# Fewer warming matmuls, and first-normalisation statistics and Newton steps regrouped in the first attention steps

## The chip, the core and the metric

The kernel runs on one core of a Trainium2 chip. Its five engines work from queues of their own and in order: PE (TensorE, matrix products), DVE (VectorE), ACT (ScalarE), POOL (GpSimd) and SP (SyncE, which here only issues transfers). The metric is the device time of one execution in microseconds (us); of several executions the median is taken, and less is better. Names such as L464 are lines of the kernel before.

## The reference

The input `x` has 16 batches of 128 tokens with 512 features. What is computed, cut to what matters:

```python
x = x + xattn(layernorm(x), ctx, ctx)      # 32 query heads, 8 key/value heads of 16
x = x + moe(layernorm(x), gate_weight, ...)# 32 experts, 8 per token, plus a shared expert

def layernorm(x):                           # over the 512 features, no weights
    return (x - mean(x)) / sqrt(var(x) + 1e-5)

def xattn(q, k, v):                         # per batch: 128 queries, 128 keys
    weights = softmax(q k^T / sqrt(16))
    return weights v
```

The mixture of experts routes every token of the second normalisation to 8 of 32 experts (sigmoid gate, groups), each with `silu(x w1) * (x w3)` times `w2`.

## The kernel before, in words

The kernel has two stages. In `attention_small` the 16 batches go through cross-attention and both normalisations; it takes roughly the first 124 us. In `experts` the tokens are routed, gathered by expert, multiplied and added to the output; it takes the rest, and in it PE is busy almost without a break.

All of PE, DVE, ACT and POOL run an order that is written out by hand: the instructions of an engine are executed in the order in which the Python code emits them, and an instruction that waits holds up all behind it on its engine.

The attention is cut into 32 items, two per batch: item `(b, i)` is half `i` of the heads of batch `b`. A loop over `n` from 0 to 31 emits one step per item. In a step PE does, in this order: the scores of item `n` (`sc`, L464, four matmuls into two PSUM tiles of which there are two buffers in all, so the scores of the next item need both exponentials of this one); the values of item `n - 1` (`oT`, L480); and transposes into one PSUM tile `x` (L434): the queries of the next batch in even steps, the second normalisation's rows in later steps, and the attention output of item `n - 2` (`oTs`). ACT takes the exponentials (`p`, L474, two per item) and copies the transposed queries out (`qT`, L455; for batches 0 and 1 DVE does that). DVE copies `oT` out (`oTs`, L489), divides by the sum of the softmax (`ri` L498, `at` L500) and so frees the tile `x`; POOL adds `at` to `x` of the batch (L507).

The first normalisation of batch `b` has three parts, which all have to be done before its queries are transposed:

- `layernorm_stats`: mean and variance on DVE, two instructions (`st` L91, `mv` L92);
- `layernorm_rstd(first, n)`: one over the square root for `n` batches at once by Newton steps, nine tiny instructions on DVE (L98 to L116) or twelve on POOL (L98 to L128);
- `rows_of`: the normalised rows `xq` on DVE (L132).

Three dictionaries say where such work is put in a step: `head[n]` ahead of the scores, `middle[n]` just ahead of the reading (on DVE and POOL) of the last set of transposes of that step, `tail[n]` at its end. The same three hold the second normalisation (its statistics of batch `b` at the end of step `2b + 4`), the keys (`keys`, ACT), and the values (`fixed_values`, two memsets of a tile `va`, and `values_of`, a copy into it).

Ahead of the loop there is the front: `x` of batch 0 is loaded in two halves, its statistics, Newton steps and rows follow on DVE (without a break between them), then its queries are transposed and step 0 begins. While this goes on, PE has no work of its own and multiplies a tile of zeros, `wz`, by itself: `keep_warm(WARM)` ahead of the first transposes, `keep_warm(FILL[-1])` between the transposes and the scores of item 0, and `keep_warm(FILL[0])` in step 0. One warming matmul (L329) is two records in the profile.

At the end of the attention, between about 106 and 124 us, the last batches pass one after the other through DVE and PE, and PE has gaps; then the experts begin.

Of the kernel before, what the change touches and what calls it, by code (L numbers as in the profile page):

```python
# [38 lines left out]
ORDER += [r for k in range(6) for r in (5 + k, 12 + k)]  # L39
ORDER += [*range(19, 29), 30, 31]  # L40
BIG = 32768
WARM = 18
FILL = {-1: 4, 0: 3}


@with_exitstack
def tile_xattn_moe(
# [15 lines left out]
    nc = tc.nc  # L63
    B, S, D = x.shape
# [24 lines left out]
    def layernorm_stats(b, norm):  # L89
        st = xnp.tile([P, 6], F32, tag="st", name="st")  # L90
        nc.vector.bn_stats(st, xs[b])  # L91
        nc.vector.bn_aggr(mv[:, norm[b], :], st)  # L92
# [58 lines left out]
    FIRST = [*range(12), *range(15, 18), 21]  # L151
# [125 lines left out]
    def attention_small():  # L277


        with ExitStack() as ph:  # L280
# [46 lines left out]
            def keep_warm(n):  # L327
                for _ in range(n):
                    nc.tensor.matmul(warm, lhsT=wz, rhs=wz, start=True, stop=True)  # L329

            keep_warm(WARM)
            nc.scalar.activation(table, table, AF.Exp)
# [63 lines left out]
            def rows_of(b):  # L396
                xqs[b] = ap2.tile([P, G, KV, HD], F32, tag="xq", name="xq")
                normalized(
                    xqs[b].rearrange("p g k d -> p k g d"),
                    xs[b].rearrange("p (k g d) -> p k g d", g=G, d=HD),  # L400
                    b,
                    FIRST,
                )
# [2 lines left out]
            layernorm_stats(0, FIRST)  # L406
            layernorm_rstd(0, 1)
            rows_of(0)
            layernorm_stats(1, FIRST)
            for i in range(2):  # L410
                keys(0, i)
            values_of(0)
# [6 lines left out]
            def transposes(*sets, pool=ps_x, between=()):  # L419


                x = pool.tile(
                    [P, 2, 2, 2, P], F32, tag=("x" if pool is ps_x else "sc"), name="x"
                )
                for s, (of, split, _) in enumerate(sets):
                    for k in range(4):
                        for h, rows in enumerate(halves):
                            if split:
                                to = x[:, h, :, s, ts(k, P // 4)]
                                by = ident[rows, rows].rearrange("p (a b) -> p a b", a=2)  # L430
                            else:
                                to = x[:, h, k // 2, s, ts(k % 2, H)]
                                by = ident[rows, rows]
                            nc.tensor.matmul(  # L434
                                to,
                                lhsT=of[rows, k, :],
                                rhs=by,
                                start=True,
                                stop=True,
                                is_transpose=True,  # L440
                                tile_position=(h * H, 0),
                            )
                for s, (_, _, then) in enumerate(sets):
                    if s == len(sets) - 1:
                        for f, a in between:
                            f(*a)
                    then(x[:, :, :, s])

            def queries(b):

                xn = xqs.pop(b).rearrange("p g k d -> p g (k d)")

                def then(x):
                    qTs[b] = ap2.tile([P, 2, 2, P], F32, tag="qT", name="qT")
                    (nc.scalar.copy if b > 1 else nc.vector.tensor_copy)(qTs[b], x)  # L455

                return xn, False, then
# [108 lines left out]
            head, middle, tail = {}, {}, {}  # L566

            def at(where, n, f, *a):
                where.setdefault(n, []).append((f, a))


            for b in (2, 3):
                at(head, 0, layernorm_stats, b, FIRST)
            at(tail, 0, layernorm_rstd, 1, 3)
            at(tail, 0, rows_of, 1)
            at(tail, 1, rows_of, 2)
            for b, n in ((4, 1), (5, 1), (6, 2), (7, 2)):
                at(tail, n, layernorm_stats, b, FIRST)
            at(head, 3, layernorm_rstd, 4, 4, nc.gpsimd)
            for b, n in zip(range(8, B), range(3, 18, 2)):  # L580
                at(middle, n, layernorm_stats, b, FIRST)
            for b in range(3, B):
                at(middle, 2 * b - 4, rows_of, b)

            at(head, 3, fixed_values, 1, nc.gpsimd)
            at(head, 4, keys, 1, 0)
            at(head, 5, keys, 1, 1)
            at(head, 5, values_of, 1)
# [20 lines left out]
            for b in range(11):  # L609
                n = min(2 * b + 13, b + 21)  # L610
# [10 lines left out]
            transposes(queries(0))  # L621
            keep_warm(FILL[-1])
            for n in range(N):
# [22 lines left out]
                else:  # L646
                    assert not between
                keep_warm(FILL.get(n, 0))
                if n in sums:
# [967 lines left out]

    pieces = [(k, i) for k in range(NTB) for i in range(NI)]
    left_over = attention_small()
    experts(pieces[1:], in_order, *left_over)  # L1620
    left = nc.values_load(
# [64 lines left out]
```

## Time and profile before

| | |
|---|---|
| median of 3 runs | 991.97 us (991.03 to 993.17) |
| the profiled execution | 985.66 us |
| its span, first to last instruction | 983.9 us |
| PE busy | 965.7 us (98%) |
| DVE, ACT, POOL busy | 288.6, 296.8, 486.7 us |
| mean granted clock of PE | 0.991 |

The profiled execution lies 6.3 us below the median of the three timed runs; sums are made against the profiled execution, and a difference found there is taken over to the median. A profile line gives an engine's instruction with its line, its output and inputs, and the number of records; in a timeline, brackets hold the idle time of the engine before it and what ended that. PEclk is the clock that was granted to PE, as a share of full speed. "<-" in a name separates what is written from what is read.

### The profile page before, as it was taken

The page shows a single profiled execution, that of the slowest core. Times are in us where ns is not written, and L with a number is a line of the kernel's source. Part 1 is how long each engine was busy: PE and PEld are TensorE (multiplying, and loading weights), DVE is VectorE, ACT ScalarE, POOL GpSimd, SP SyncE. Part 2 cuts the span into 40 slices and gives each one's busy share as a digit, 9 for nine tenths or more (in the row PEclk, how much of TensorE's full clock was granted, in tenths as well). Part 3 has the DMA queues.
Part 4 walks back from the last instruction along what each step waited for, and adds up shares of the span by engine and source line. Part 5 has one row for each costly group of instructions (what it writes and reads, how often), then busy time and mean ns, then how long its engine had stood idle before and what let it go on. Part 6 is the DMA issues. An engine that isn't in the chain of part 4 may idle for free.

```text
span 983.9 us, 13941 instructions
## 1 busy us (share of the span) xinstructions
PE 965.7 (98%) x4985; PEld 548.5 (56%) x4985; DVE 288.6 (29%) x972; ACT 296.8 (30%) x468; POOL 486.7 (49%) x597
## 2 busy tenths in 40 slices
PE   9999899999999999999999999999999999999996
PEld 5344444547666556666666676767654444444453
DVE  7877778961121111111112111111121112111100
ACT  6788513412222222222222222222222222222221
POOL 3577244753454446444547454545463444555443
PEclk9999799999999999999999999999999999999998
DMA  9011206145666658676769676757685776677543
GB/s 322 15 44 44 76 2 215 43 156 157 131 152 135 164 121 201 159 159 132 180 134 222 131 180 129 181 129 179 135 209 123 170 180 159 146 167 167 114 65 46
DMA packets 59869, 137.15 MB, mean 139 GB/s; under 512 B 12168, under 2 KB 16392, under 8 KB 59792
## 3 DMA queue, kind: packets, MB, share of 16 engines
q0 software_dynamic: 32032, 69.25, 37.9%
q1 hardware_dynamic: 27680, 66.81, 20.0%
q8 instruction: 41, 0.67, 0.3%
q14 instruction: 36, 0.29, 0.1%
q10 hardware_dynamic: 80, 0.13, 0.0%
HBM read 96.71 MB, written 46.73 MB: 146 GB/s over the span
## 4 chain that ended last, share of the span: by engine, by line
PE 84%; issue 5%; POOL 4%; DMA 3%; DVE 2%; ACT 1%; POOLq 0%; ACTq 0%; DVEq 0%
PE gu L1494 41%; PE y L1548 21%; PE gu L258 6%; PE trx L1446 4%; PE sc L464 4%; DMA out_dram<-yw,token 3%; POOL out_dram L1520 3%; PE oT L480 3%; PE y L1339 2%; PE x L434 2%; PE tok L1006 1%; DVE st L91 0%; PE lg L556 0%; PE lgT L541 0%; DMA x<-in_x_dram 0%
## 5 line engine op out<-in xcount | busy, mean ns | idle before, releaser
L1494 PE MATMUL gu<-xnT,wup 128*128 128x256 f32 (+27 forms) x1664 | 490.5, 444 | 0.0
L1494 PEld LDWEIGHTS gu<-xnT,wup 128*128 128x128 f32 x1664 | 314.4, 190 | 192.9 <-issue 133.5
L1520 POOL DMA_INDIRECT out_dram<-yw,token x150 | 234.8, 1565 | 347.3 <-ACT yw L1557 237.7
L1548 PE MATMUL y<-wdn,sa 128*128 128x512 f32 (+2 forms) x672 | 263.3, 599 | 0.0
L1505 DVE TENSOR_TENSOR sa<-sl,gu 128x256 f32<-128x256 f32 (+27 forms) x104 | 52.2, 502 | 623.6 <-PE gu L1494 618.3
L1557 ACT ACTIVATE yw<-y,wt 128x512 f32<-128x512 f32 x138 | 94.9, 687 | 243.8 <-PE y L1548 206.1
L1422 POOL DMA_INDIRECT xg<-rows,token x138 | 142.3, 1031 | 46.6 <-issue 27.8
L1548 PEld LDWEIGHTS y<-wdn,sa 128*128 128x128 f32 (+2 forms) x672 | 98.0, 170 | 94.4 <-issue 85.0
L1503 ACT ACTIVATE sl<-gu 128x256 f32<-128x256 f32 (+27 forms) x104 | 46.7, 449 | 250.2 <-PE gu L1494 250.2
L474 ACT ACTIVATE p<-sc 128x1024 f32<-128x1024 f32 x64 | 62.1, 1024 | 14.5 <-PE sc L464 14.5
L1462 ACT COPY xnT<-trx 128x512 f32<-128x512 f32 x69 | 37.2, 589 | 89.8 <-PE trx L1446 89.8
L258 PE MATMUL gu<-xnT,sup 128*128 128x512 f32 x128 | 60.5, 615 | 0.7 <-ACT ssl L266 0.7
L1000 POOL TENSOR_SCALAR hq<-slice_q,sq 128x138 f16<-128x138 f16 x32 | 35.2, 1113 | 36.3 <-DVE sq L1305 20.1
L1446 PEld LDWEIGHTS trx<-ident,xg 64*128 64x128 f32 x1104 | 37.2, 138 | 17.8 <-issue 17.5
L464 PE MATMUL sc<-qT,kz 32*128 32x512 f32 x256 | 43.9, 640 | 0.2 <-ACT p L474 0.2
L1446 PE MATMUL trx<-ident,xg 64*128 64x64 f32 x1104 | 42.1, 226 | 0.0
L1462 DVE COPY xnT<-trx 128x512 f32<-128x512 f32 x57 | 39.3, 689 | 5.6 <-PE trx L1446 4.8
L507 POOL TENSOR_TENSOR x<-x,at 128x256 f32<-128x256 f32 x29 | 21.3, 739 | 38.2 <-DVE at L500 36.0
L258 PEld LDWEIGHTS gu<-xnT,sup 128*128 128x128 f32 x128 | 23.4, 194 | 25.0 <-issue 22.5
L480 PE MATMUL oT<-p,va 128*32 128x512 f32 x256 | 34.3, 608 | 2.0 <-DVE oTs L489 2.0
L1477 DVE SCALAR_TENSOR_TENSOR own<-expert,owner,xg 128x32 f32<-128x32 f32 x138 | 31.2, 245 | 0.0
L1339 PE MATMUL y<-sdn,sa 128*128 128x512 f32 x64 | 29.6, 597 | 0.0
(190 smaller groups left out, 462.6 us busy)
## 6 DMA issues: line engine op xcount, KB each, us to landing
wup<-in_w_dram SPq DMA_DIRECT2D x64, 512.0 KB, 5.2
wdn<-in_w_dram SPq DMA_DIRECT2D x32, 512.0 KB, 5.1
rows<-xn SPq DMA_DIRECT2D x16, 256.0 KB, 2.0
out_dram<-x SPq DMA_DIRECT2D x16, 256.0 KB, 2.3
x<-in_x_dram SPq DMA_DIRECT2D x15, 256.0 KB, 5.6
out_dram<-yw,token POOLq DMA_INDIRECT x150, 5.0
xg<-rows,token POOLq DMA_INDIRECT x138, 4.4
cTs<-in_cT_dram SPq DMA_DIRECT2D x4, 256.0 KB, 4.6
```

The costliest lines, as they stand in the source:

```text
L258: nc.tensor.matmul(acc, lhsT=sup[:, w, d, ts(i, P)], rhs=xnT[k][:, d, :], start=(d == 0), stop=(d == ND - 1),)
L464: nc.tensor.matmul(scs[j // 2][:, j % 2], lhsT=kzs[b // 4 % 2][rows, b % 4, i, :], rhs=qT[rows], start=True, stop=True, tile_position=(j * ...
L474: nc.scalar.activation(p, sc, AF.Exp, scale=1.0 / HD**0.5)
L480: nc.tensor.matmul(oT[j * HP : (j + 1) * HP], lhsT=vas[b // 4 % 2][:, b % 4, 2 * j + i, :], rhs=ps.pop((b, i, j)), start=True, stop=True, ...
L1422: nc.gpsimd.indirect_dma_start(out=t, out_offset=None, in_=rows[:, :], in_offset=bass.IndirectOffsetOnAxis(ap=token[:, j : j + 1], axis=0) ...
L1446: nc.tensor.matmul(trs[s // 2][:, h, s % 2, d, :], lhsT=xg[j][rows_of_half, ts(d, P)], rhs=ident[rows_of_half, rows_of_half], start=True, ...
L1462: copy(xnT[n % NTB][:, :, col : col + P].rearrange("p d (h t) -> p h d t", h=2), tr)
L1494: nc.tensor.matmul(acc[:, 0:m], lhsT=wup[k % NW][:, w, d, ts(i, P)], rhs=xnT[n % NTB][:, d, 0:m], start=(d == 0), stop=(d == ND - 1),)
L1505: nc.vector.tensor_tensor(acts[n % NTB][:, i, 0:m], banks[2][:, 0:m], acc[:, 0:m], ALU.mult)
L1520: ins = nc.gpsimd.indirect_dma_start(out=flat, out_offset=bass.IndirectOffsetOnAxis(ap=token2[:, k - 1 : k] if a else token[0:b, j : j + 1 ...
L1548: nc.tensor.matmul(y[c0:c1, :], lhsT=acts[n % NTB][:, i, col : col + c1 - c0], rhs=wdn[pieces[n][0] % NW][:, i, :], start=(i == 0), stop=( ...
L1557: nc.scalar.activation(yws[j], y, AF.Copy, scale=wt[:, j : j + 1])
```

## The change

Four things are changed, all in the front and the first eight steps of the attention:

- `WARM` goes from 18 to 15 and `FILL[-1]` from 4 to 2.
- Statistics of the first normalisation: batch 1 moves from the front (between the rows of batch 0 and the copy of its queries) to the head of step 0, behind that copy; those of the batches after it, two to a step before, are spread, mostly one to a step.
- Newton groups: before, batches 1 to 3 on DVE at the end of step 0 and 4 to 7 on POOL at the head of step 3. Now batches 1 and 2 on DVE at the end of step 0, 3 and 4 on POOL at the head of step 2, and 5 to 7 on POOL at the head of step 5. (Groups after that, at step 10 and later, stay.)
- The rows of batch 3 move from step 2 to step 3, and the two memsets of the second `va` tile on POOL from the head of step 3 to the head of step 1.

```diff
-WARM = 18
-FILL = {-1: 4, 0: 3}
+WARM = 15
+FILL = {-1: 2, 0: 3}
...
             layernorm_stats(0, FIRST)
             layernorm_rstd(0, 1)
             rows_of(0)
-            layernorm_stats(1, FIRST)
             for i in range(2):
                 keys(0, i)
...
-            for b in (2, 3):
+            for b in (1, 2):
                 at(head, 0, layernorm_stats, b, FIRST)
-            at(tail, 0, layernorm_rstd, 1, 3)
+            at(tail, 0, layernorm_rstd, 1, 2)
             at(tail, 0, rows_of, 1)
             at(tail, 1, rows_of, 2)
-            for b, n in ((4, 1), (5, 1), (6, 2), (7, 2)):
-                at(tail, n, layernorm_stats, b, FIRST)
-            at(head, 3, layernorm_rstd, 4, 4, nc.gpsimd)
-            for b, n in zip(range(8, B), range(3, 18, 2)):
+            for b in (3, 4):
+                at(tail, 1, layernorm_stats, b, FIRST)
+            at(head, 2, layernorm_rstd, 3, 2, nc.gpsimd)
+            at(tail, 2, layernorm_stats, 5, FIRST)
+            for b, n in zip(range(6, B), (3, 4, 5, 7, 8, 9, 11, 13, 15, 17)):
                 at(middle, n, layernorm_stats, b, FIRST)
+            at(head, 5, layernorm_rstd, 5, 3, nc.gpsimd)
             for b in range(3, B):
-                at(middle, 2 * b - 4, rows_of, b)
-
-            at(head, 3, fixed_values, 1, nc.gpsimd)
+                at(middle, max(2 * b - 4, 3), rows_of, b)
+
+            at(head, 1, fixed_values, 1, nc.gpsimd)
```

In the built program DVE has the same instructions in the attention as before, in another order; PE has five warming matmuls less; POOL has one Newton group, twelve instructions, more.

## The prediction

> **What bounds the kernel now.** I read the page's busy shares first. PE is busy 98% of the span and the chain that ended last runs through PE for 84% of it. A saving in another engine therefore counts only where PE stands idle for it. The change touches only the front and steps 0 to 7 of the attention, so I next asked where PE is idle there, in the table of windows (columns: stretch, its length, then busy time and records of PE, PEld, DVE, ACT, POOL, then PEclk, DMA share, GB/s):
>
> ```profile
> 0.57:3.98 3.41, 2.89 (x13) 2.90 (x14) 1.57 (x6) 1.49 (x2) 2.79 (x15) 1.00 0.51 152
> 3.98:7.40 3.42, 2.76 (x25) 2.57 (x23) 2.79 (x13) 1.01 (x2) 1.62 (x15) 1.00 0.93 286
> ...
> 20.00:28.00 8.00, 7.29 (x76) 3.03 (x80) 7.19 (x17) 6.32 (x9) 5.50 (x18) 1.00 0.58 232
> 30.00:34.00 4.00, 4.00 (x32) 1.24 (x30) 3.47 (x10) 2.88 (x4) 0.73 (x1) 1.00 0.02 4
> 106.38:109.80 3.42, 1.47 (x24) 0.41 (x19) 3.11 (x13) 0.43 (x2) 1.68 (x1) 1.00 0.17 65
> 109.80:113.21 3.41, 3.17 (x32) 2.38 (x28) 2.88 (x8) 1.29 (x3) 2.58 (x2) 0.50 0.26 94
> ...
> 205.37:208.78 3.41, 2.52 (x13) 1.13 (x12) 3.41 (x13) 1.75 (x2) 0.80 (x2) 1.00 0.23 89
> ```
>
> From 30 us on PE is never idle; between 20 and 28 us it is, by 0.71 us, while DVE is nearly full. The last three rows matter for the clock: after a stretch of 3.42 us with PE busy 1.47 (43%) the clock fell to half; after one with 2.52 (74%) it did not. The first two rows show the clock opening: 13 warming records in 2.89 us (0.22 us each), then 24 or 25 in 2.76 (0.11 each), although the column says 1.00 in both.
>
> Then the timeline, PE first, DVE and POOL after it, shows which waits these are:
>
> ```profile
> 1.09 5.65 PE L329 MATMUL warm<-wz 128*128 128x128 f32 x36 [1.09 <-DVE wz L198]
> 7.59 0.47 PE L434 MATMUL x<-ident,xq 64*128 64x64 f32 x8 [0.86 <-DVE xq L132]
> 7.99 1.16 PE L329 MATMUL warm<-wz 128*128 128x128 f32 x8
> 9.08 1.14 PE L464 MATMUL sc<-qT,kz 32*128 32x512 f32 x8
> ...
> 22.99 0.46 PE L434 MATMUL x<-ident,xq 64*128 64x64 f32 x8 [0.24 <-DVE at L500]
> ...
> 26.24 0.47 PE L434 MATMUL x<-ident,oTs 64*128 64x64 f32 x8 [0.48 <-DVE at L500]
> ```
> ```profile
> 8.09 0.18 DVE L92 BATCH_NORM_AGGREGATE mv<-st 128x2 f32<-128x6 f32 x1
> 8.19 0.66 DVE L455 COPY qT<-x 128x512 f32<-128x512 f32 x1
> ...
> 24.35 1.13 DVE L132 TENSOR_SCALAR xq<-x,mv,rstd 128x512 f32<-128x512 f32 x1 [0.63 <-POOL rstd L128]
> ```
> ```profile
> 24.12 0.20 POOL L128 TENSOR_TENSOR rstd<-h,r 128x4 f32<-128x4 f32 x1
> 24.25 0.95 POOL L354 MEMSET va<- 128x1024 f32 x1
> ```
>
> DVE stands 0.63 us until POOL has finished its Newton group of four batches, and then its rows take 1.13 us, not the 0.55 of the other rows, beside POOL's memset. PE's waits of 0.24 and 0.48 us for `at` hang on DVE's queue there. All idle time of PE from the first warming matmul to 30 us, the 0.86 in the front included, is 2.0 us (1.3 in the stretch from 7.40 to 30, the rest ahead of it). That caps what the change can bring.
>
> **The parts, one by one.**
>
> *Warming ahead of the transposes, 18 to 15.* Six records less at 0.112 us: PE stops at 6.07, not 6.74. The first transposes wait for the rows (6.90 to 7.46), so the wait grows from 0.86 to 1.5 us and nothing is gained here: 0. It gains where the clock opens later than 3.98. If it is still slow at 7.40, 18 matmuls have done 29.6 of 36 records at 0.213, the other 6.4 end at 8.1, and the transposes are 0.5 late; 15 end at 7.5 and are not late. So 0 to -0.5; I take -0.1, since only openings after about 6.2 count.
>
> *Warming ahead of the first scores, 4 to 2, with the statistics of batch 1 moved.* Four records less, 0.45 us. The last warming record starts at 8.87 and the scores follow at 9.08, although `qT` was there at 8.85; `qT` itself began at 8.19, behind the aggregate of batch 1. Without both: transposes end at 8.06, the copy starts about 0.05 later (8.11), ends at 8.77, and PE follows a DVE result after 0.14 (7.46 to 7.59): scores at 8.91. -0.17, on the path.
>
> *Statistics of 1 and 2, Newton of 1 and 2 on DVE.* DVE does two statistics, nine Newton instructions (0.195 us apart, the same for two columns as for three) and the rows, as before, from 8.68 instead of 8.76: rows of batch 1 end at 12.74 instead of 12.82. PE wants them at 13.3 less 0.17. Cost 0; cover 0.35 us.
>
> *Statistics one a step.* Ahead of `at` of step 3, DVE now has statistics 5 and 6 instead of 6, 7 and 8, but the rows of batch 3, formerly in step 2, stand there. From the first `oT` of batch 1 (PE ends it at 19.98): `oTs` from 20.05, pitch 0.60; statistics 0.79; rows 0.46; `ri` 0.27; `at` 0.42: end at 22.59 instead of 22.84, all less the 0.17. PE's `oT` ends at 22.76 less 0.17. So the wait of 0.24 goes.
>
> *Newton of 3 and 4 on POOL.* Statistics 3 and 4 end where 4 and 5 ended, 17.58 less 0.17; twelve instructions 0.285 us apart make 3.4: ready at 20.9, wanted by the rows at 21.3. The 0.63 wait and the 0.58 of stretching go. `at` of step 4 then ends near 25.2, before PE's `oT` (25.76 less 0.41): PE's 0.48 goes as well. But the scores after it need the second exponential, which ended at 26.80 and moves only by 0.41, to 26.4; with a score pair of 1.07 the step ends at 27.5 instead of 27.99. So of the 0.48 only some 0.07 stays: what is late next is the exponential.
>
> *Newton of 5 to 7 on POOL, step 5.* This adds a wait. POOL reaches it after adding `at` of step 4, at about 26.0, and ends at 29.4; the rows of batch 5, at 29.66 before, are due at 29.2. DVE stands 0.2 to 0.3 us, with `ri`, `at` and the copies behind it; POOL's copy into `va` (0.62) comes right after and may stretch the rows by up to 0.4 (a row at 24.35 was stretched by 0.58). Cover: 0.32 us of DVE idle ahead of `ri` at 30.52, and PE takes `at` only 0.6 us after its end there. I take 0; without the cover +0.3.
>
> *Memsets of `va` on POOL, now behind its constants.* These end at 5.87; 0.95 us, then the small one from about 6.92, just as the rows of batch 0 start at 6.90, on the path. Its own time is 0.09 (on DVE) to 0.32 (on POOL). 0 to +0.35; I take +0.1.
>
> Sum: -0.10 - 0.17 - 0.24 - 0.07 + 0.10 = -0.48. The profiled execution of 985.66 becomes 985.2; the median of 991.97, 6.3 above it, becomes 991.5. The experts' stage, bound by PE, hands the shift on unchanged. About 0.2% (2.0 us) is what a measurement of this kernel tells from no change; the three timed runs alone lie 2.1 apart.
>
> The Trainium skill, "TensorE: Matmul & The Clock Gate", Part 1, says that PE's clock opens after about 3.4 us of sustained work and falls back only after an idle window of that length, the windows running free. By that rule the longer pause of 1.5 us costs nothing and the sum stays -0.48. The rows above speak against it: the clock fell after a window that was 43% busy.
>
> **Rivals.**
>
> *The clock closes in the front (slower).* With 15 matmuls PE is busy 2.09 us of the window 3.98 to 7.40: 61%, between the 43% that closed it and the 74% that did not. If it closes at 7.40, the first scores cost 1.07 more, fills and transposes some 0.3: +1.4, with the gain +0.9, 992.9. If it stays for a second window, as at 109.80, another score pair of 1.07: +2.0, 994.0. It decides from a threshold above 61%. For it: nearer evidence is lacking; against: 61% is nearer to the 74%, and the edges lie elsewhere in other executions. Chance 0.14.
>
> *The gain is eaten by POOL.* The Newton group of 5 to 7 and the memset both turn up at their upper bounds (+0.3 and +0.25 over what I took): 991.9 to 992.1. For it: POOL has twelve instructions more, and my due time and ready time lie 0.2 apart the wrong way. Chance 0.20.
>
> *The shift meets the later closing better (faster).* The clock steps at 109.80 and 120.04 lie 31 and 34 windows of 3.413 us after 3.98, so it switches on a grid. Of three half-speed windows after the attention one may fall away when the gap at 107 to 109 us moves or the executions differ: a window of some 3.2 us busy at half clock is worth 1.6, with the gain -2.1: 989.9. It is as likely to go the other way in single runs. Chance 0.11.
>
> **How the numbers follow.** My forecast has 0.55: 991.5. Its bounds are -1.2 (late opening -0.5, and the front's memset at nothing, and a little more of the 0.48) and +0.3, to which the runs' own scatter of 1.1 either way adds. The range reaches to 989.8, where the faster rival lies, and to 993.4, past the clock closing for one window. Faster by over 0.2% needs under 990.0: 0.09 from the forecast by scatter, 0.02 from POOL's case, 0.09 from the grid: 0.20. Slower needs over 994.0: 0.03, 0.04, and 0.09 from the clock: 0.16. The rest is 0.64.
>
> **What would show it.** After: scores of item 0 at 8.9; no wait of DVE for `rstd` at step 4 and no row of 1.13 us there; no wait of PE for `at` at 23 and 26 us; a short wait of DVE for `rstd` near 29 us; PE without a gap from there; the scores of step 8 (32.31 before) near 31.9. Wrong would be: PEclk 0.5 before 15 us, rows of batch 0 longer than 0.9 us, or PE waiting for `at` near 32 us.

## The result: 0.15% faster, just below the range

| | before | after |
|---|---|---|
| median of 20 executions each | 990.85 us (987.47 to 993.19) | 989.12 us (986.51 to 993.14) |
| mean of the 20 | 990.76 | 989.37 |
| the profiled execution | 985.66 | 990.59 |
| its span | 983.9 | 988.7 |
| mean granted clock of PE in it | 0.991 | 0.990 |

The ratio of after to before is 0.9985 (95% interval 0.9974 to 0.9995), about 1.5 us; the means lie 1.4 us apart, the medians 1.7. The forecast was 991.5 with a range from 989.8; the measured median lies 0.7 below its foot. The sign was right, the size (-0.48) was not.

The profiled execution of after is not a typical one: at 990.59 it lies in the upper part of its twenty. So the traces are compared stage by stage and not by their ends.

**The front and the first steps, after.** The timeline of PE, to be read against that of before (lines of after are numbered one lower):

```profile
1.09 6.12 PE L329 MATMUL warm<-wz 128*128 128x128 f32 x30 [1.09 <-DVE wz L198]
7.28 0.47 PE L433 MATMUL x<-ident,xq 64*128 64x64 f32 x8
7.68 0.71 PE L329 MATMUL warm<-wz 128*128 128x128 f32 x4
8.62 1.14 PE L463 MATMUL sc<-qT,kz 32*128 32x512 f32 x8 [0.23 <-DVE qT L454]
...
22.30 0.46 PE L433 MATMUL x<-ident,xq 64*128 64x64 f32 x8
...
25.14 0.46 PE L433 MATMUL x<-ident,oTs 64*128 64x64 f32 x8
25.53 1.76 PE L463 MATMUL sc<-qT,kz 32*128 32x512 f32 x8
...
28.22 0.47 PE L433 MATMUL x<-ident,xq 64*128 64x64 f32 x8
```

The brackets of 0.24 and 0.48 us "<-DVE at" are gone at 22.30 and 25.14. The scores of item 6, which took 1.35 us before, take 1.76: they start earlier and wait inside for the second exponential. Scores of item 0 come 1.34 us after the first transposes (8.62 less 7.28); before it was 1.49 (9.08 less 7.59). In this execution 30 warming records last until 7.2 us, where the 36 of before stopped at 6.74, because the clock opened only at 6.38.

The timeline of DVE and that of POOL, the same stretch:

```profile
6.59 0.55 DVE L132 TENSOR_SCALAR xq<-x,mv,rstd 128x512 f32<-128x512 f32 x1
...
23.78 0.52 DVE L132 TENSOR_SCALAR xq<-x,mv,rstd 128x512 f32<-128x512 f32 x1
...
29.21 0.80 DVE L132 TENSOR_SCALAR xq<-x,mv,rstd 128x512 f32<-128x512 f32 x1 [0.17 <-POOL rstd L128]
```
```profile
5.77 0.95 POOL L354 MEMSET va<- 128x1024 f32 x1
6.78 0.44 POOL L355 MEMSET va<- 128x32 f32 x1
...
28.98 0.19 POOL L128 TENSOR_TENSOR rstd<-h,r 128x3 f32<-128x3 f32 x1
29.12 0.61 POOL L358 COPY va<-cn 128x512 f32<-128x512 f32 x1
```

DVE no longer stands at step 4 and the rows of 1.13 us there are 0.52. The new wait for the group of 5 to 7 is there, 0.17 us, with rows of 0.80 behind it. The rows of batch 0 take 0.55 beside the small memset, as they did without it.

The table of windows (stretch, its length, busy us and records of PE, PEld, DVE, ACT, POOL, then PEclk, DMA share, GB/s):

```profile
20.00:28.00 8.00, 7.99 (x72) 2.88 (x72) 7.49 (x20) 6.96 (x10) 4.13 (x13) 1.00 0.51 206
30.00:34.00 4.00, 4.00 (x33) 1.17 (x32) 3.40 (x10) 3.38 (x4) 1.71 (x3) 1.00 0.00 0
105.37:108.78 3.41, 1.46 (x26) 0.47 (x20) 3.10 (x13) 0.41 (x2) 1.61 (x1) 1.00 0.16 59
108.78:112.19 3.41, 3.31 (x34) 2.38 (x28) 2.82 (x8) 1.22 (x3) 2.64 (x2) 0.50 0.25 94
...
221.42:224.83 3.41, 0.92 (x4) 0.84 (x5) 0.69 (x1) 1.07 (x2) 1.14 (x2) 1.00 0.80 300
224.83:228.24 3.41, 3.41 (x9) 2.73 (x9) 0.00 (x0) 0.38 (x1) 0.00 (x0) 0.50 0.28 85
```

Between 20 and 28 us PE is busy 7.99 us, 7.29 before. At the end of the attention the half clock comes again, after a window 43% busy, as before.

**Where the profiled time went.** The scores of step 16 start at 55.26 (56.19 before), and the first routed matrices of the experts were still to come when a stall put this execution back. The timeline of PE and that of ACT there:

```profile
223.91 5.41 PE L1495 MATMUL gu<-xnT,wup 128*128 128x256 f32 x16 [3.86 <-ACT xnT L1463]
```
```profile
222.78 1.07 ACT L1463 COPY xnT<-trx 128x512 f32<-128x512 f32 x2 [14.65 <-remote]
```

PE waits 3.86 us for ACT, and ACT, DVE and POOL all start again within 0.3 us of 222.8, released by a signal whose sender the profile does not know ("<-remote"); the window before it was 27% busy, so one at half clock follows. It cost 5.8 us: at the ninth record of the shared expert this execution was 0.95 ahead of before's (124.94 against 125.89), at the end 4.85 behind. None of the sixteen later traces has it, ten of them with the regrouping, so I count it as no part of the change; what sent the signal stays open. The twenty executions of either kernel lie some 5 us above the later ones of the same kernel (990.85 against 985); whether most of them had such a stall no trace shows.

### The profile page after: what moved, and what is told of

Same layout as the page of the kernel before. It is cut to its first block, busy times and chain, and to the rows that moved or that the text cites. A ratio compares the mean times of both kernels' runs of the same rounds, so it can differ in the third digit from the quotient of the medians.

```text
span 988.7 us, 13933 instructions
## 1 busy us (share of the span) xinstructions
PE 968.0 (98%) x4975; PEld 549.7 (56%) x4975; DVE 289.1 (29%) x972; ACT 296.6 (30%) x468; POOL 488.7 (49%) x609
## 4 chain that ended last, share of the span: by engine, by line
PE 86%; issue 4%; POOL 3%; DMA 3%; another core or an unknown queue 1%; DVE 1%; ACT 1%; POOLq 0%; ACTq 0%; DVEq 0%
PE gu L1495 42%; PE y L1549 21%; PE gu L258 6%; PE sc L463 4%; PE trx L1447 4%; PE oT L479 3%; DMA out_dram<-yw,token 3%; POOL out_dram L1521 3%; PE x L433 2%; PE y L1340 1%; PE tok L1007 1%; PE lg L555 0%; PE lgT L540 0%; ACT p L473 0%
## 5 line engine op out<-in xcount | busy, mean ns | idle before, releaser
L258 PE MATMUL gu<-xnT,sup 128*128 128x512 f32 x128 | 60.4, 614 | 0.7 <-ACT ssl L266 0.7
L1463 DVE COPY xnT<-trx 128x512 f32<-128x512 f32 x57 | 39.3, 689 | 31.9 <-PE y L1549 21.8
L258 PEld LDWEIGHTS gu<-xnT,sup 128*128 128x128 f32 x128 | 23.4, 194 | 25.0 <-issue 22.3
```

The costliest lines, as they stand in the source:

```text
L258: nc.tensor.matmul(acc, lhsT=sup[:, w, d, ts(i, P)], rhs=xnT[k][:, d, :], start=(d == 0), stop=(d == ND - 1),)
L1463: copy(xnT[n % NTB][:, :, col : col + P].rearrange("p d (h t) -> p h d t", h=2), tr)
```

## Experiments

From one series to the next the median of before differs (990.85 above, 984.87 to 985.91 below), so each result is compared with runs of before in its own series, on the same chip. "Filled" kernels have more warming matmuls at the end of the attention (the edit of e4). From each trace's timeline I took five marks: when the clock opened; how much later than its rows allow the first transposes began ("late"; rows' end and 0.14); transposes to first scores; scores of item 2 to scores of item 16; and the "gap", from the scores of item 30 to the ninth record of the shared expert (`gu`, L258). From there to the end every trace takes the same time to within 0.4 us (858.0), but for the stall above. "1 + 1" means two half-clock windows with an open one between them.

| | opened | late | transposes to scores | item 2 to 16 | gap | half-clock windows in the gap |
|---|---|---|---|---|---|---|
| before | 3.98 | 0 | 1.49 | 41.50 | 25.30 | 3 |
| after | 6.38 | 0 | 1.34 | 41.03 | 25.30 | 3 |
| e1 after | 6.15 | 0 | 1.35 | 41.03 | 24.94 | 1 + 1 |
| e2 warming only | 4.33 | 0 | 1.39 | 41.48 | 23.64 | 1 |
| e3 regrouping only | 6.63 | 0.76 | 1.49 | 41.04 | 26.55 | 1 + 2 |
| e4 after, filled | 5.72 | 0 | 1.33 | 41.04 | 22.58 | 0 |
| e5 before, filled | 7.31 | 0.99 | 1.48 | 41.49 | 22.58 | 0 |
| e6 regrouping, filled | 5.75 | 0 | 1.48 | 41.04 | 22.59 | 0 |
| e7 after, filled | 6.39 | 0 | 1.34 | 41.03 | 22.59 | 0 |
| e10 before | 5.15 | 0.01 | 1.48 | 41.48 | 24.25 | 1 |
| e11 after | 4.96 | 0 | 1.34 | 41.04 | 25.78 | 2 |
| e12 warming, filled | 7.18 | 0.20 | 1.35 | 41.48 | 22.58 | 0 |
| e13 before, filled | 6.13 | 0.23 | 1.48 | 41.49 | 22.58 | 0 |
| e14 after, filled | 4.14 | 0 | 1.34 | 41.05 | 22.59 | 0 |
| e15 before | 5.94 | 0.31 | 1.48 | 41.50 | 25.71 | 2 |
| e16 after | 3.94 | 0 | 1.34 | 41.02 | 23.90 | 2 |

### The two halves of the change, and its end (first series)

**e1** is after, unchanged, for a second trace. **e2** is before with the warming of after (statistics of batch 1 stay in the front), **e3** is after with the warming of before:

```diff
 e2, on before                     e3, on after
-WARM = 18                        -WARM = 15
-FILL = {-1: 4, 0: 3}             -FILL = {-1: 2, 0: 3}
+WARM = 15                        +WARM = 18
+FILL = {-1: 2, 0: 3}             +FILL = {-1: 4, 0: 3}
```

**e4** is after with warming matmuls in the gap at the end of the attention, meant to keep the clock from closing there. This filling is used in several runs below:

```diff
             gate_parts(8)
+            warm = ps_sc.tile([P, 2, TB], F32, tag="sc", name="warm2")[:, 0, 0:P]
+            keep_warm(8)
             values(*items[N - 1])
...
             gate_sums(8, nc.scalar.copy)
+            warm = gu[:, 1, 0:P]
+            keep_warm(5)
             transposes(turn_of(12), turn_of(13))
```

> The changed kernel as it is. Theory A (the gain is made in the front and in steps 3 to 7 of the attention and handed on unchanged): from the first statistics of batch 0 to the scores of step 16 it is 0.5 to 0.7 us shorter than in the kernel before, and no more is gained later; the ratio of times is 0.9990 to 0.9995. Theory B (much of the 1.7 us between the medians comes from how many windows at half clock an execution has): ratio anywhere from 0.997 to 1.001, and executions with the same mean granted clock differ by under 1 us between the kernels.

> Kernel before, with only 15 and 2 warming matmuls. Theory A: the scores of item 0 start 0.05 to 0.1 us earlier against the end of batch 0's rows where the clock opens early (the aggregate of batch 1 still stands ahead of the copy of the queries), 0.2 to 0.5 more where it opens after 5.7 us; the waits for Newton at step 4 stay. Mean gain 0.2 to 0.3 us. Theory B: no difference beyond the number of half-clock windows. The clock-closing rival: PEclk 0.5 somewhere between 7 and 15 us.

> Changed kernel with 18 and 4 warming matmuls. Theory A: scores of item 0 near where the kernel before has them; from step 2 to step 16 it gains 0.4 to 0.5 us, since the 0.24 and 0.48 us waits of PE for the division are gone. Theory B: no difference beyond the number of half-clock windows.

> Changed kernel with 8 warming matmuls more after the gate's partial products of batch 8 and 5 more ahead of the transposes of batches 12 and 13, where PE stood idle between 106 and 114 us. It measures what the half clock there costs. Theory B (half-clock windows are worth 1.2 to 1.7 us each): the three windows at half clock after the attention are gone, mean clock up by 0.005, and it is 2 to 4 us faster than the changed kernel. Against it: if DVE and ACT set the end there, the clock comes back and under 1 us is gained.

Measured, against 984.87 for before: e1 983.54, ratio 0.9983 (0.9972 to 0.9993), the result once more. e2 984.64, 0.9997 (0.9986 to 1.0007). e3 984.77, 1.0000 (0.9990 to 1.0010). e4 982.10, 0.9969 (0.9957 to 0.9981). Two expectations were missed: e1's gain is larger than Theory A's 0.9990 to 0.9995, and e4 is 1.4 us faster than e1, not 2 to 4.

Neither half alone could be told from before by its median, and yet the traces show both at work: the regrouping takes items 2 to 16 in 41.02 to 41.09 (e8) instead of 41.48 to 41.50 in every kernel that has it, and the shorter filling brings the first scores 0.10 to 0.15 sooner. Each half's trace shows what ate its share. In e3 the 18 matmuls, with the clock open only at 6.63, made the transposes 0.76 late. In e2 the first values came late; the timeline of ACT, then that of PE:

```profile
9.87 0.62 ACT L358 COPY va<-cn 128x512 f32<-128x512 f32 x1 [2.13 <-DMA cn<-in_c_dram]
10.39 1.93 ACT L474 ACTIVATE p<-sc 128x1024 f32<-128x1024 f32 x2
```
```profile
11.46 2.04 PE L464 MATMUL sc<-qT,kz 32*128 32x512 f32 x8 [0.77 <-ACT p L474]
```

The copy of the values stands ahead of the first exponential on ACT, and its transfer landed at 9.87 (8.64 before): PE waited 0.77 us for the exponential instead of 0.24. The edit does not touch the transfers or their order, so I take this for their scatter; it is also the next thing that would be late if the front were made shorter still. The gap (23.6 to 26.6 us) moves the time more than any part of the change; in e4, where it is 22.58, the trace has no half-clock window there.

### Before and the regrouping without the clock's windows (second series)

**e5** is before, **e6** is after with the warming of before, **e7** after, all with the filling. **e8** tries for more on e7: `WARM = 14`, and the copy of the first values on POOL instead of ACT.

```diff
 e8, on e7
-WARM = 15
+WARM = 14
...
-                (nc.gpsimd.tensor_copy if k else nc.scalar.copy)(
+                nc.gpsimd.tensor_copy(
```

> Kernel before with the 8 and 5 warming matmuls in the gap at the end of the attention, so that the half-clock windows there are gone and only the first 30 us differ from the next two kernels. Theory C (the regrouping is worth a fixed 0.47 us, the shorter warming 0.15 us in every execution and up to 0.8 more where the clock opens late; what goes beyond that between the medians are half-clock windows at the attention's end): 2 to 3 us faster than before, and 0.7 to 0.9 us slower than the changed kernel with the same filling. Theory D (the change itself is worth 1.3 to 1.7 us in every execution, whatever the windows do): 1.3 to 1.7 us slower than that one.

> Changed kernel with 18 and 4 warming matmuls, and with the filling of the gap. Theory C: 0.47 us faster than the kernel before with the filling, 0.2 to 0.4 us slower than the changed kernel with it; executions whose clock opens late lie 0.5 to 0.8 above the others. Theory D: no such split.

> Changed kernel with the filling of the gap (the kernel of run e4_keep_clock, to be compared with the other two on one chip). Theory C: 0.7 to 0.9 us faster than the kernel before with the filling, with the least scatter of the three. Theory D: 1.3 to 1.7 us faster.

> Changed kernel with the filling, 14 warming matmuls ahead of the transposes, and the copy of the first values on POOL, which has nothing to do from 7.3 to 17 us, instead of ACT, where it stands ahead of the first exponentials and waited for the values' load until 8.6 to 9.9 us. If that load is what is late next: 0.1 to 0.3 us faster than the changed kernel with the filling, more in executions with a late load. If not: the same within 0.1 us.

Measured, against 984.93: e5 983.20, 0.9981 (0.9972 to 0.9990); e6 982.91, 0.9981 (0.9973 to 0.9990); e7 982.53, 0.9982 (0.9973 to 0.9991); e8 982.33, 0.9977 (0.9967 to 0.9987).

By their ratios the three cannot be told apart. The medians of e5 and e7 are 0.67 apart, just short of Theory C's 0.7 to 0.9, and the means only 0.25; e6 lies between them by medians, 0.29 below e5 and 0.38 above e7. Both kernels have executions on a higher level (two of e5's eleven near 984.5, five of e7's twelve at 983.8 to 986.2); without these the medians are 983.01 and 982.23, 0.78 apart, but that leaves out more of e7 than of e5. The higher executions have a mean granted clock of 0.994 to 0.996, most others 0.997 or 0.998: the filling seems not to keep the clock open in every execution, and no trace shows one in which it failed. e5 gained 1.7 us by the filling, less than the 2 to 3 expected. The timeline of PE in e5 shows the cost of the three warming matmuls more:

```profile
1.09 7.24 PE L329 MATMUL warm<-wz 128*128 128x128 f32 x36 [1.09 <-DVE wz L198]
8.26 0.46 PE L434 MATMUL x<-ident,xq 64*128 64x64 f32 x8
```

The rows were ready at 7.13 (`xq` from 6.58 for 0.55), the transposes started at 8.26: the 36 records were in the way, some 29 of them (6.22 us at 0.213) before the clock opened at 7.31. No line puts a wait there, because PE is busy; only the distance from the end of `xq` shows it. e8 is 0.20 below e7 by medians, within the expected 0.1 to 0.3 but not to be told from nothing by the intervals, and its trace shows a loss: POOL's copy of the values made items 0 to 2 take 5.78 us instead of 5.60.

### Does the clock close in the front? (third series)

**e9** goes on in the direction of the change, on e7: `WARM = 10`, and no filling matmuls at all in the front. **e10** and **e11** are before and after once more. **e12** is e2 with the filling at the end of the attention.

```diff
 e9, on e7
-WARM = 15
-FILL = {-1: 2, 0: 3}
+WARM = 10
+FILL = {-1: 0, 0: 0}
```

> Changed kernel with the filling of the gap, with 10 warming matmuls ahead of the transposes and none between them and the second scores. PE is then idle from at most 5.5 us to 7.3. If the clock follows how busy the window before was, with a threshold somewhere between 43% and 74%, it is at half speed for one or two windows between 5 and 15 us (or has not opened), the scores of items 0 and 1 take 2.1 us instead of 1.07 per group, and the kernel is 1 to 3 us slower than the changed kernel with the filling (about 0.9990 to 1.0005 of the kernel before). If short pauses do not matter to the clock, it is as fast as that one or 0.1 us faster.

> The kernel before once more, for another opening of the clock. Theory C: the first transposes start at the later of the end of the rows plus 0.14 us and 4.78 us plus 0.476 times the time at which the clock opens (36 records, 0.213 us apart before it and 0.112 after it); from step 2 to step 16 the same 41.50 us as in the first profile.

> The changed kernel once more, on another chip, for the size of the whole. Theory C with the windows at the end of the attention: ratio 0.998 to 0.9995 (0.9 us from the first 30 us, and 0 to 1 us from fewer half-clock windows). First transposes at the end of the rows plus 0.14 us, whenever the clock opens before 6.9; step 2 to step 16 41.03 us.

> Kernel before with only the warming shortened (15 and 2), and the filling of the gap. Theory C: between the kernel before and the changed kernel, both with the filling: 0.3 to 0.5 us faster than the one, 0.4 to 0.5 us slower than the other; about 0.9975 to 0.998 of the kernel before.

Measured, against 985.05: e9 985.79, 1.0012 (1.0002 to 1.0021); e11 983.78, 0.9986 (0.9977 to 0.9995); e12 982.68, 0.9974 (0.9963 to 0.9985); e10 984.25, one execution.

e9 lost all that filling and regrouping had gained. The windows of its front, then its PE timeline:

```profile
6.14:9.55 3.41, 1.25 (x16) 0.69 (x16) 2.62 (x8) 1.96 (x3) 0.74 (x2) 1.00 1.09 349
9.55:12.97 3.42, 2.33 (x10) 1.01 (x8) 2.65 (x12) 1.94 (x2) 0.00 (x0) 0.50 1.00 344
12.97:16.38 3.41, 3.41 (x22) 0.70 (x16) 0.69 (x1) 1.94 (x2) 0.00 (x0) 0.50 1.08 383
```
```profile
8.76 1.35 PE L463 MATMUL sc<-qT,kz 32*128 32x512 f32 x8 [0.88 <-DVE qT L454]
11.20 2.99 PE L463 MATMUL sc<-qT,kz 32*128 32x512 f32 x8 [1.09 <-ACT p L473]
```

After a window 37% busy the clock closed, and it stayed closed for a second one, after a window of 68%. Items 0 to 2 took 7.77 us instead of 5.60. So the slower rival names a real mechanism, at 2.2 us for two windows in this execution (it had priced them at 2.5 ahead of the gain). At 984.29 it is the second fastest of e9's ten; the median lies 1.5 above it, and the ratio above the expected 1.0005. What the slower executions paid more no trace shows.

In the traces of after it does not happen. The windows of e16 have the clock's edge where before's profile had it, the case that the rival priced:

```profile
3.94:7.35 3.41, 2.11 (x19) 1.92 (x17) 2.84 (x12) 1.26 (x2) 2.69 (x17) 1.00 0.91 269
7.35:10.77 3.42, 3.11 (x26) 1.96 (x26) 2.67 (x8) 1.54 (x3) 0.00 (x0) 1.00 1.09 366
```

2.11 us of 3.41 are 62% (it had said 2.09), and the clock stayed open. In all seven traces of after, filled or not, the clock opening anywhere from 3.94 to 6.39, it never closed in the front.

e12, with the clock open as late as 7.18, was 0.20 late where 18 matmuls were 0.99 late at 7.31 (e5).

### Where the last half microsecond lies (fourth series)

**e13** repeats e5 and **e14** repeats e7, on one chip; **e15** and **e16** are single executions of before and after beside them. The question was whether the change is worth the same with and without half-clock windows at the end of the attention.

> Kernel before with the filling of the gap, again. Theory C (0.9 us from the first 30 us, the rest of the 1.4 in the gap): 0.9 us slower than the changed kernel with the filling. Rival E (all 1.4 us come from the first 30 us): 1.4 us slower.

> Changed kernel with the filling of the gap, again. Theory C: 0.9 us faster than the kernel before with the filling. Rival E: 1.4 us.

> Kernel before, one trace. Theory C: first transposes at the later of the end of the rows plus 0.14 and 4.78 plus 0.476 times the opening of the clock; the gap (from the scores of item 30 to the ninth record of the shared expert's products after it) 22.6 us plus 1.0 to 1.7 for each half-clock window.

> Changed kernel, one trace. Theory C: first transposes at the end of the rows plus 0.14 unless the clock opens after 6.9; the gap as for the kernel before, by its half-clock windows.

Measured, against 985.91: e13 983.45, 0.9982 (0.9972 to 0.9991); e14 982.00, 0.9962 (0.9947 to 0.9976). e15 986.15 and e16 983.52. The marks of e15 came as expected; e16's gap, 23.90 with two half-clock windows, is shorter than the 24.6 or more expected of two.

The pair is 1.45 apart by medians, as Rival E had it (1.4), where the pair of the second series was 0.67 apart, as Theory C had it: e14's six executions all lie within 0.21 us, e13's spread from 982.7 to 984.6. One pair is thus not enough; all executions of these kernels in the four series together, as means in us with their standard errors (and the number of executions), give

| | unfilled | filled |
|---|---|---|
| before | 985.33 ± 0.12 (111) | 983.53 ± 0.13 (23) |
| warming of after | 984.81 ± 0.23 (12) | 982.95 ± 0.23 (11) |
| regrouping of after | 985.08 ± 0.34 (12) | 983.10 ± 0.18 (11) |
| both | 983.87 ± 0.14 (24) | 982.61 ± 0.20 (27) |

With the filling the parts add up: -0.58 for the warming and -0.43 for the regrouping make -1.01, and both together measure -0.92 (standard error 0.24); the difference of 0.09 has an error of about 0.4. Without it they make -0.77 (-0.52 and -0.25), but -1.46 (0.18) together; that difference of 0.69 has an error of about 0.45, so it is not shown that they fail to add up. The gain without filling is larger by 0.54 with an error of 0.30. These errors take the executions as independent, which the levels below and the two unlike pairs put in doubt. About half a microsecond of the gain thus perhaps comes from the windows at the end of the attention. The traces do not show it: the gaps of before (25.30, 24.25, 25.71) and of after (25.30, 24.94, 25.78, 23.90) overlap. This part stays open.

**A version faster than both** came out of it: after with the filling (e4, e7, e14), at ratios of 0.9969, 0.9982 and 0.9962 to before.

## Why the prediction was right in sign and short in size

**The foot it stood on.** The forecast took off 0.48 from 991.97, the median of three executions. Twenty gave 990.85, so 1.1 of the 2.4 us by which the forecast missed were there before any change. Its bounds, -1.2 and a scatter of 1.1 around 991.97, reach to 989.7, and the range was ended at the faster rival's 989.8; three executions did not bound their own median, whose error was 1.1.

**18 to 15: the term of -0.10 was mis-sized.** The mechanism is as stated (a clock that opens late leaves slow matmuls in the way), and its step that failed is "only openings after about 6.2 count". That came from the one profile of before, where the rows of batch 0 ended at 7.46 and the clock opened at 3.98. The step took that opening, and that end of the rows, as typical. In all but one of the other traces the rows ended 0.1 to 0.45 earlier (e6: 0.08 later), and the opening lay anywhere between 3.94 and 7.31, as a clock switching on a grid of 3.41 us would have it. The seven traces with 18 matmuls were late by 0, 0.01, 0, 0.23, 0.31, 0.76 and 0.99, on average 0.33; of those with 15 only e12 was late, by 0.20. So the term is about -0.3, and its bound, given as -0.5, is at least -0.8. Where the rows end near 7.15, an opening of 5.15 cost nothing (e10), one of 5.94 cost 0.31 (e15) and one of 7.31 cost 0.99 (e5): on the line through the last two, openings count from about 5.3 on (an estimate), not 6.2.

**4 to 2, with the statistics moved: -0.17, measured -0.15** (1.49 to 1.34, to within 0.01 in every trace of before and of after). The size was right. Scores follow `qT`, which follows the transposes without the aggregate between them; but the shorter filling alone, with the aggregate still there, already brings 0.09 to 0.14 (e2 1.39, e12 1.35), and the moved statistics alone bring nothing (e3 and e6, 1.48 to 1.49).

**Step 3: -0.24, measured -0.23.** The wait is gone and from the scores of item 2 to those of item 5 it is 8.71 us instead of 8.94.

**Step 4: -0.07, and then a wait that was not in the sum.** As the prediction said, the exponential is next late: the scores of item 6 end only 0.23 nearer to those of item 2, though PE's 0.48 is gone: that is what step 3 had given, so step 4 itself gave nothing to this point. But by the end of the scores of item 7 the difference is 0.52, and 0.46 of it stays. The timeline of before has the reason, in a line that the prediction did not use:

```profile
29.15 0.46 PE L434 MATMUL x<-ident,xq 64*128 64x64 f32 x8 [0.17 <-PE oT L480]
```

The timeline of DVE has the end of `at` ahead of it, before and then after:

```profile
28.58 0.42 DVE L500 TENSOR_TENSOR at<-x,ri 128x256 f32<-128x256 f32 x1
```
```profile
27.38 0.42 DVE L499 TENSOR_TENSOR at<-x,ri 128x256 f32<-128x256 f32 x1
```

The profile puts this wait down to PE's own `oT`. But DVE's `at`, which frees the tile `x`, ran from 28.58 to 29.00, and the transposes follow its end by 0.15, about the distance at which PE followed DVE at 7.46 (0.14). So I take it that the releaser named is not the one that counted; with `at` ending at 27.80 in after, the wait is gone (28.22, no bracket). The step that failed here is the sum's end at step 4: it left out this wait of 0.17, and the regrouping's -0.31 became about -0.46 (between 0.43 and 0.48 less in every trace with it).

**Newton of 5 to 7: 0, measured 0.** DVE stood 0.17 us (0.2 to 0.3 forecast), the rows were stretched by 0.25 (up to 0.4), and PE has no gap at 30 to 34 us: the cover held. The scores of step 8, forecast near 31.9, start at 31.32; 0.31 of that comes from batch 0, whose rows ended 0.31 earlier in this execution (their statistics began at 3.80 instead of 4.23).

**Memset beside the rows of batch 0: +0.10, measured 0.** The rows took 0.55 in after (0.58 at most, in e3); it was the small memset that was stretched, to 0.44 from 0.32. The Trainium skill, "GPSIMD Engine Reference", section 8, says that POOL shares its SBUF interfaces with DVE, with contention for DVE instructions in a 2-port mode or with two SBUF inputs; whether the rows are of either kind no run shows. The rows of 0.80 beside POOL's copy agree with it; the rows of 0.55 beside the small memset show that sharing alone does not tell who pays.

**The sum of the first 30 us** is then -0.3 - 0.15 - 0.46, about -0.9 instead of -0.48, and the filled kernels measure -0.92, pooled over two unlike pairs and e4. Of the 2.4 us by which the forecast missed, 1.1 are thus the foot and 0.4 these terms; the other 0.8 no trace assigns to anything. They lie within the scatter: -0.9 is inside the result's interval (-0.5 to -2.6).

**The rivals.** POOL did not eat the gain. In the front the clock did not close in any trace of after, though a window was only 62% busy in e16. But the rival's ground, a threshold of the busy share, does not hold: a window of 57% (e10) left the clock open and one of 58% (e1) closed it, and in e2 a window of 43%, the share that closed it in before, left it open, while the next, of 52%, closed it:

```profile
106.72:110.14 3.42, 1.46 (x16) 0.23 (x13) 3.14 (x12) 0.42 (x2) 1.93 (x1) 1.00 0.20 77
110.14:113.55 3.41, 1.79 (x32) 1.45 (x28) 3.06 (x8) 1.51 (x4) 2.33 (x2) 1.00 0.27 102
113.55:116.96 3.41, 3.29 (x26) 1.83 (x27) 2.99 (x13) 2.59 (x6) 0.00 (x0) 0.50 0.16 57
```

So the seven traces of after show that the clock stayed open there, and not how near it came to closing. The rule of the Trainium skill, "TensorE: Matmul & The Clock Gate", Part 1, that only an idle window of some 3.4 us brings the clock down, does not hold here: windows 37% to 58% busy did. The third rival, a better meeting with the later closing, was the nearest in time (989.9); its mechanism may account for the half microsecond left open (0.54, error 0.30), not for a whole window of 1.6.

## What to carry to other kernels

Before a term is sized from one trace, ask which of its inputs vary from execution to execution: here the moment at which PE's clock opened and the arrival of the first tile decided whether three matmuls cost nothing or 0.8 us, and both were taken from one profile. A wait put down to the engine's own last instruction can be a wait for another engine that ended just before; compare the ends of all that it needs. And when parts are worth less than the scatter, remove the source of the scatter (here by filling the gap, so that the clock mostly stayed open) and measure the parts there: they added up to within 0.1 us, though with an error of 0.4.

## What was not expected of the hardware

- The end of the attention costs 1.3 us (after) to 1.8 us (before) more than it must: 16 and 10 warming records in PE's gaps (e7's timeline has `warm` from 106.29 for 2.05 us) bring the gap from 23.6 to 26.6 us down to 22.58 or 22.59 in every trace, without a half-clock window in any of them. By the gap's excess over 22.58, one such window costs 0.65 us (e16, mean of two) to 1.7 (e10).
- The busy share of a window does not say whether the clock closes after it (43% did in before and did not in e2), nor whether it opens: the half-clock window of after at 108.78 was 97% busy (3.31 of 3.41) and two more followed, while one of 85% (2.89) in before's front was enough.
- Executions of one kernel fall into levels rather than scatter evenly: those of before on one chip lay near 983.9, 984.8, 986.0 and 987.6.
